# Taking a chunk's sums out of PSUM at the fifth multiplication of the next chunk

## The chip, the cores and the metric

The kernel runs on one core of a Trainium2 chip. A core has five engines with a queue each: PE multiplies matrices, DVE (VectorE) and ACT (ScalarE) work on elements, POOL (GpSimd) here mostly issues gathers, and SP (SyncE) issues transfers. An engine works through its own queue in the order in which the program was written. The metric is the device time in microseconds (us); lower is better.

## The reference

The reference is one layer of a graph network on 6250 nodes with 256 features and 200,000 edges, followed by a mixture of experts and two normalizations. Cut to what matters:

```
h    = x * rsqrt(max(deg_out, 1))                       # every node's row, scaled
m    = segment_sum(h[src], dst) * rsqrt(max(deg_in, 1)) # sum over the edges into each node
x1   = m @ W_gc + b_gc + x @ W_res + b_res
core = top-2 mixture of 64 experts (256 -> 512 -> 256, gelu) of x1
y    = batch-normalized (x1 + core)
out  = layer-normalized (x + y)
```

The edges come sorted by `dst`, and small destinations have many more edges than large ones. The change sits in the `segment_sum`.

## The kernel before, in words

The program first counts degrees, then multiplies `x` by both weights, and keeps the scaled product in SBUF as `hrow`: 50 tiles (`NT`) of 125 nodes, with a value's rounded half in the first 256 columns and the rest in the second 256. Then comes the stage that the change is in, here called the sweep. It sums `hrow` over the edges, in two ways that are written into one another.

**Dense chunks.** The first 1101 groups of 128 edges (`GD`) are split into 30 chunks (`ND`). A chunk covers a window of 128 destination nodes. For a chunk the kernel makes a table of how often each source node occurs for each destination of the window, as follows. DVE makes one-hot tiles from the edge lists, for eight groups at a time: `lo` (L637), `lo` times `worth` with a third part (L642, L643), and `hotk` (L650); all but the `worth` product show as L248, the helper that compares. They are made while the eight groups before are being counted, at the second, fourth and sixth of those (`making`, L652). PE counts a group with one small multiplication `pc<-hotk,lo` (L671), ACT puts a bank of counts into `words` (L655, a "put"), DVE adds the one column that may already hold a count (L706, an "add", written two puts later), and ACT unpacks `words` into `counts` in six pieces (L661, a "cast", of 1024 or 1152 columns). Then PE multiplies `counts` with `hrow`, 50 multiplications of 128 x 512 into one PSUM bank (L715). While chunk c is multiplied, chunk c+1 is counted. The 50 multiplications are the clock of the written order: t goes from 0 to 49 in each chunk, and everything else is placed by t. The six casts for chunk c+1 stand at t = 41, 43, 46 and 48 of chunk c and at t = 1 and t = 4 of chunk c+1 (L879).

**The two banks.** `banks` holds two PSUM banks (`sm`, L597), and chunk c multiplies into bank c % 2. When a chunk's 50 multiplications are done, its sums are taken out into `resd`: ACT scales the second 256 columns into `resd` (L728), DVE scales the first 256 and adds the two (L729), and SP writes `resd` to `z_dram` (L591, in `sums_done`). The bank that is not being multiplied into also serves two small jobs of the same chunk: at t = 20 turned rows of finished nodes go into it (L773) at t = 32 their logits (L782; both earlier and twice in the last two chunks), and at t = 30 a row of totals (L724), which ACT writes into the last two columns of a new `resd` (L725). The totals come from `row_raw`, which SP loads at t = 1 (L718) and DVE turns at t = 24 (L720).

**Gathered chunks.** The other 462 groups of edges are done by fetching 128 rows of `h_dram` each (POOL, L574, a ring of eight buffers), a one-hot tile from DVE (L909) and two multiplications (L579, L580) into a third bank, which ACT copies to `resg` (L932) and SP writes out. They are spread evenly over the written order.

**Finished nodes.** Every chunk also reads back two tiles of nodes whose sums are complete: SP loads `z` and `xr` after t = 20 (L172), DVE makes `x` from them in the next chunk from t = 10 on (L755, L759, L760, L763), PE turns them at t = 20 (L773).

All of the sweep is written by hand under a manual schedule: nothing reorders an engine's instructions. After the sweep come the routing, the 64 experts and the two normalizations, which the change does not touch.

Of the kernel before, what the change touches and what calls it, by code (L numbers as in the profile page):

```python
# [16 lines left out]
AF = mybir.ActivationFunctionType  # L17
ALU = mybir.AluOpType
# [10 lines left out]
NT = N // TP  # L29
D = 256  # L30
# [102 lines left out]
ND = len(DENSE)  # L133
# [21 lines left out]
def gnn_moe_kernel(ctx, tc, x_in, src, dst, bases, nexts, firsts, parts, lasts, runs, W_gc, b_gc, W_res, b_res, Wg, bg, w1, b1, w2, b2,  # L155
                   gamma, beta, out):
    nc = tc.nc
    V, S, G, T = nc.vector, nc.scalar, nc.gpsimd, nc.tensor
# [62 lines left out]
    with tc.tile_pool(name="edges", bufs=1) as ep, ExitStack() as later:  # L221
# [9 lines left out]
        okc = ep.tile([128, ND], F32, name="okc")  # L231
# [29 lines left out]
        with tc.tile_pool(name="late", bufs=1) as lp, tc.tile_pool(name="both", bufs=2) as bp, \  # L261
# [65 lines left out]
            for k, values in enumerate((LOW, HIGH)):  # L327
                c = 0
# [225 lines left out]
        with tc.tile_pool(name="xs", bufs=1) as xs, tc.tile_pool(name="hotg", bufs=2) as hg, \  # L554
# [32 lines left out]
            def sums_done(res, c):  # L587

                row = nc.values_load(base_i[0:1, c:c + 1], engines=(SP_E,), min_val=0, max_val=N,
                                     skip_runtime_bounds_check_because="at most N")  # L590
                nc.sync.dma_start(out=z_dram[ds(row, WIN), :], in_=res)  # L591

            ends_met = {}
            live = {"carry": []}


            banks = [ps_s.tile([128, 512], F32, name=f"sm{i}") for i in range(2)]  # L597
# [114 lines left out]
            def multiply(c, t):  # L712

                sm, ok = banks[c % 2], okc[:, c:c + 1]
                T.matmul(sm, counts[:, t, :], hrow[:, t, :], start=(t == 0), stop=(t == NT - 1))  # L715
                if t == 1:
                    for b in range(3):
                        nc.sync.dma_start(out=row_raw[b * NU:(b + 1) * NU, :], in_=words[c % 2][TP + b:TP + b + 1, :, :])  # L718
                if t == 24:
                    V.tensor_scalar(row_sums, row_raw, -WORD, None, op0=ALU.add)  # L720
                if t == 30:
                    live["resd"] = rsp.tile([WIN, D + 2], F32, name="resd")
                    by = banks[(c + 1) % 2][:, 2 * D - 2:]
                    T.matmul(by, row_sums, two, start=True, stop=True)  # L724
                    S.activation(live["resd"][:, D:], by, AF.Copy, scale=ok)  # L725
                if t == NT - 1:
                    res = live["resd"]
                    S.activation(res[:, :D], sm[:, D:], AF.Copy, scale=ok)  # L728
                    V.scalar_tensor_tensor(res[:, :D], sm[:, :D], ok, res[:, :D], op0=ALU.mult, op1=ALU.add)  # L729
                    ends_met["dense"] = res  # L730
                    if c < ND - 1:
                        sums_done(res, c)

            def last_rows():

# [111 lines left out]
            def dense():  # L847
# [27 lines left out]
                for c in range(ND):  # L875
                    for t in range(NT):
                        for us, g in todo.get(NT * c + t, []):
                            yield us, lambda g=g: count(g)
                        for at, p in ((41, 0), (43, 1), (46, 2), (48, 3), (51, 4), (54, 5)):  # L879
                            d = c + 1 if at < NT else c  # L880
                            if t == at % NT and 0 < d < ND:
                                yield 0.0, lambda d=d, p=p: apart(d, cuts[p], cuts[p + 1])
                        if c == 0 and t % 2 == 0 and made_of < NT:
                            yield 1.0, lambda t=made_of: halves(t)
                            made_of += 2
                            if made_of > NT:
                                yield 0.0, lambda: first_rows()
                        if c == 0 and t == 45:
                            yield 0.0, lambda: left_edges()
                        yield 0.22, lambda c=c, t=t: multiply(c, t)  # L890
                        if 10 <= t < 46:
                            yield 0.04, lambda c=c, t=t: x_step(c, t)
# [70 lines left out]
            with tc.For_i(0, n_groups, 1) as gi:  # L963
# [6 lines left out]
                                op1=ALU.mult)  # L970
# [3 lines left out]
                                       op0=ALU.mult, op1=ALU.add)  # L974
# [22 lines left out]
                with tc.For_i(0, n_win, 1):  # L997
# [9 lines left out]
                    res = rsp.tile([WIN, D + 2], F32, name="res_e", tag="resg")  # L1007
# [82 lines left out]
    with tc.tile_pool(name="xw", bufs=1) as xw, tc.tile_pool(name="xl", bufs=3) as xl, \  # L1090
# [42 lines left out]
        with tc.manual_schedule():  # L1133
# [11 lines left out]
            for t0, z in sums.items():  # L1145
# [7 lines left out]
                for t in range(t0, t0 + n):  # L1153
                    V.scalar_tensor_tensor(x[:, t, :], z[:, t - t0, :D], s_in[:, t - t0:t - t0 + 1], x[:, t, :],
                                           op0=ALU.mult, op1=ALU.add)
# [75 lines left out]
    with tc.tile_pool(name="ps_r", bufs=1, space=PSUM) as ps_r, tc.manual_schedule(engines={PE_E}):  # L1231
# [45 lines left out]
        while n > 2:  # L1277
# [6 lines left out]
                               op1=ALU.mult, accum_out=slots_of)  # L1284
# [285 lines left out]
    with tc.tile_pool(name="fin", bufs=1) as fp, tc.tile_pool(name="gat", bufs=7) as gp, \  # L1570
# [10 lines left out]
        for t0 in range(0, NT, 2):  # L1581
            yr = gp.tile([TP, 2, 2, D], F32, name="yr")
            node_dma(nc.sync, True, yr.rearrange("p t j d -> p t (j d)"), node_rows(y_rows, t0, 2))
            for t in range(t0, t0 + 2):
                for j in range(2):
                    V.scalar_tensor_tensor(x[:, t, :], yr[:, t - t0, j, :], gates[:, j, t:t + 1], x[:, t, :],  # L1586
                                           op0=ALU.mult, op1=ALU.add)
# [23 lines left out]
        scale = fp.tile([TP, D], F32, name="scale")  # L1611
# [121 lines left out]
```

## Time and profile before

| what | us |
|---|---|
| three runs | 1549.29, 1552.34, 1556.32 |
| their median | 1552.34 |
| the profiled execution | 1550.04 |
| span of its instructions | 1548.3 |
| the sweep's 30 chunks, first multiplication to last | about 203 to 912 of the span |

The profiled execution lies 2.3 us below the median, and 1.7 us of it lie outside the span. A row of the timeline gives the start, the duration, the engine, the line, what is written from what, the number of instructions merged into the row, and in brackets how long the engine stood idle before and what ended that. A row of the waits gives who waited for whom, the sum in us, the number of times and the longest. The views that the prediction rests on are shown there.

### The profile page before, as it was taken

Reading aid. Unit: us, or ns where it says so; the run is one execution under the profiler, and the core shown is the slowest. Engines: PE = TensorE matmul, PEld = TensorE weight load, DVE = VectorE, ACT = ScalarE, POOL = GpSimd, SP = SyncE. Lnnn points to the kernel's source line nnn. Section 1 sums busy time; section 2 is a strip of 40 time slices with the busy share of each in tenths; the row PEclk is TensorE's granted clock in tenths of the full one; section 3 lists DMA queues with packets and bytes.
Section 4 is the critical chain, followed back from the end, with each engine's and each line's share of the span. In section 5 each row is a group of like instructions: output and inputs, shape, how many; then the busy total and the mean of one; then the engine's idle time right before and its main releaser. Section 6 shows DMA issues by size and latency. Waiting matters only on the chain. (4 is left out here: it accounts for less than half of the span.)

```text
span 1548.3 us, 27873 instructions
## 1 busy us (share of the span) xinstructions
PE 1370.5 (89%) x8598; PEld 1024.6 (66%) x8598; DVE 978.0 (63%) x2430; ACT 637.9 (41%) x1531; POOL 813.8 (53%) x878
## 2 busy tenths in 40 slices
PE   4999648888899999999999866599999999997995
PEld 2555325556677777777777644588788887886652
DVE  8999878877777877666666538632233223222887
ACT  2343353344465455555555431422222233332247
POOL 5100005777777777777777720256566676663000
PEclk8999858999999999999999975799999999999997
DMA  6789776777878888878787829378789798785934
GB/s 169 225 261 282 223 234 203 198 213 208 233 224 234 231 239 235 231 220 235 229 238 230 242 77 204 92 224 288 213 254 308 229 304 262 247 269 166 236 81 146
DMA packets 215784, 341.92 MB, mean 221 GB/s; under 512 B 23741, under 2 KB 149303, under 8 KB 215627
## 3 DMA queue, kind: packets, MB, share of 16 engines
q1 hardware_dynamic: 159351, 180.34, 40.0%
q0 software_dynamic: 49376, 152.63, 33.8%
q10 hardware_dynamic: 6900, 7.08, 1.6%
q8 instruction: 71, 1.16, 0.3%
q14 instruction: 86, 0.70, 0.2%
HBM read 258.97 MB, written 73.81 MB: 215 GB/s over the span
## 5 line engine op out<-in xcount | busy, mean ns | idle before, releaser
L574 POOL DMA_INDIRECT r<-h_dram,srcg x462 | 503.4, 1090 | 207.2 <-issue 64.3
L715 PE MATMUL sm<-hrow,counts 125*128 125x512 f32 x1500 | 509.1, 430 | 3.4 <-ACT counts L661 3.4
L715 PEld LDWEIGHTS sm<-hrow,counts 125*128 125x128 f32 x1500 | 256.3, 195 | 29.7 <-issue 9.1
L655 ACT ACTIVATE words<-pc 128x136 f32 (+15 forms) x436 | 139.8, 321 | 290.9 <-PE pc L671 275.3
L1433 ACT ACTIVATE hT<-ph,b1c 128x128 f32<-128x128 f32 (+3 forms) x256 | 108.3, 423 | 296.8 <-PE ph L1431 274.5
L671 PE MATMUL pc<-hotk,lo 128*128 128x136 bf16 (+10 forms) x1101 | 183.3, 252 | 48.2 <-DVE hotk L248 42.3
L1431 PE MATMUL ph<-xgT,w1s 128*128 128x128 f32 (+8 forms) x1024 | 207.0, 348 | 0.8 <-DVE xgT L1416 0.8
L1468 PE MATMUL py<-w2s,hT 128*128 128x256 f32 (+1 forms) x800 | 191.9, 383 | 0.0
L661 ACT CAST counts<-words 125x1152 fp32r<-125x1152 uint8 (+1 forms) x180 | 190.7, 1084 | 1.1 <-DVE words L706 1.1
L1431 PEld LDWEIGHTS ph<-xgT,w1s 128*128 128x128 f32 x1024 | 170.9, 192 | 28.8 <-issue 8.6
L1392 POOL DMA_INDIRECT y_dram<-ys,dest x124 | 120.3, 970 | 116.8 <-DVE ys L1446 59.3
L1392 POOL DMA_INDIRECT xg<-x_dram,ids x124 | 121.4, 979 | 102.3 <-DVE ids L1348 64.8
L671 PEld LDWEIGHTS <-lo 128*128 128x128 bf16 x1101 | 74.2, 103 | 133.1 <-issue 90.8
L579 PE MATMUL pg<-r,hot 128*128 128x258 f32 x462 | 146.0, 316 | 18.1 <-DMA r<-h_dram,srcg 17.0
L1468 PEld LDWEIGHTS py<-w2s,hT 128*128 128x128 f32 (+1 forms) x800 | 144.2, 188 | 20.2 <-issue 0.3
L1446 DVE TENSOR_TENSOR ys<-py,b2s 128x256 f32<-128x256 f32 (+3 forms) x124 | 52.4, 423 | 164.6 <-PE py L1468 138.9
L580 PE MATMUL pg<-r,hot 128*128 128x256 f32 x462 | 130.3, 282 | 0.0
L1416 DVE COPY xgT<-pte 128x256 f32<-128x256 f32 (+8 forms) x64 | 38.5, 601 | 135.9 <-PE pte L1414 135.9
L248 DVE TENSOR_TENSOR hotk<-key,iota 128x1088 bf16<-128x1088 bf16 (+10 forms) x138 | 118.9, 862 | 2.6 <-issue 2.6
L579 PEld LDWEIGHTS pg<-r,hot 128*128 128x128 f32 x462 | 88.4, 191 | 41.1 <-DMA r<-h_dram,srcg 28.6
L248 DVE TENSOR_TENSOR lo<-lo_b,iota 128x1000 bf16<-128x1000 bf16 x138 | 93.3, 676 | 28.1 <-PE pc L671 25.8
L428 PE MATMUL pr<-wcat,fT 128*125 128x512 f32 x200 | 102.5, 637 | 3.5 <-DMA wcat<-in_L_gnn_W_res_dram 2.7
(337 smaller groups left out, 1859.5 us busy)
## 6 DMA issues: line engine op xcount, KB each, us to landing
w1s<-in_L_gnn_w_dram SPq DMA_DIRECT2D x64, 512.0 KB
w2s<-in_L_gnn_w_dram SPq DMA_DIRECT2D x64, 512.0 KB
y_dram<-zeros SPq DMA_DIRECT2D x48, 256.0 KB
yr<-y_dram SPq DMA_DIRECT2D x25, 448.0 KB
b2s<-in_L_gnn_b_dram SPq DMA_DIRECT2D x64, 128.0 KB
r<-h_dram,srcg POOLq DMA_INDIRECT x462
h_dram<-hrow SPq DMA_DIRECT2D x5, 1344.0 KB
z_dram<-zeros ACTq DMA_DIRECT2D x7, 903.0 KB
```

The costliest lines, as they stand in the source:

```text
L248: V.tensor_tensor(o, pairs(t, c0, n, m), iota_2[:, None, :m, :].to_broadcast([128, n // 2, m, 2]), ALU.is_equal)
L574: G.indirect_dma_start(out=f32(r[:, :2 * D]), out_offset=None, in_=h_dram[:, :], in_offset=bass.IndirectOffsetOnAxis(ap=idx, axis=0))
L579: T.matmul(pg, hot, r[:, D:], start=first, stop=False)
L580: T.matmul(pg[:, :D], hot, r[:, :D], start=False, stop=last)
L655: return S.activation(to, pc, AF.Copy, bias=WORD)
L661: S.copy(counts[:, t0:t1, :], each[:TP, u:u + t1 - t0, :, b])
L671: T.matmul(pc, los[g // PAIRS][:, r // 2, :, r % 2], hots[g // PAIRS][:, r // 2, :NU * w, r % 2], start=(i == 0), stop=(i == k - 1))
L715: T.matmul(sm, counts[:, t, :], hrow[:, t, :], start=(t == 0), stop=(t == NT - 1))
L1392: w = G.indirect_dma_start(**kw)
L1431: T.matmul(ph[:, :m], w1s[:, kk, c * 128:(c + 1) * 128], xgT[:, kk, :m], start=(kk == 0), stop=(kk == 1))
L1433: S.activation(hT[:, c, :m - apart], ph[:, :m - apart], AF.Gelu, bias=b1_e[:, c:c + 1])
L1468: T.matmul(py[:n], hT[:, c, k * 128:k * 128 + n], w2s[:, c, :], start=(c == 0), stop=(c == 3))
```

## The change

The three steps that take a chunk's sums out (ACT, DVE, SP) become a function `taken`. It is called for chunk c-1 right behind the fifth multiplication (t = 4) of chunk c, and for the last chunk behind its own last multiplication as before. The work itself is the same.

```diff
-                if t == NT - 1:
-                    res = live["resd"]
-                    S.activation(res[:, :D], sm[:, D:], AF.Copy, scale=ok)
-                    V.scalar_tensor_tensor(res[:, :D], sm[:, :D], ok, res[:, :D], op0=ALU.mult, op1=ALU.add)
-                    ends_met["dense"] = res
-                    if c < ND - 1:
-                        sums_done(res, c)
+                if t == 4 and c:
+                    taken(c - 1)
+                if (c, t) == (ND - 1, NT - 1):
+                    taken(c)
+
+            def taken(c):
+                sm, ok, res = banks[c % 2], okc[:, c:c + 1], live["resd"]
+                S.activation(res[:, :D], sm[:, D:], AF.Copy, scale=ok)
+                V.scalar_tensor_tensor(res[:, :D], sm[:, :D], ok, res[:, :D], op0=ALU.mult, op1=ALU.add)
+                ends_met["dense"] = res
+                if c < ND - 1:
+                    sums_done(res, c)
```

In the changed kernel the ACT step is L733 and the DVE step L734; lines behind them are five higher than before. The end of chunk 24 (counting from 0) shows what moves. ACT's queue there before, with casts (L661) and puts (L655) around the step that fills `resd` from the bank `sm`:

```order
L655 ACTIVATE words0_2914<-pc_11102 128x17x14
L661 CAST counts_2916<-words1_2915 125x1152
L661 CAST counts_2916<-words1_2915 125x1024
L728 ACTIVATE resd_11024<-sm0_2944,okc_93 128x256
L655 ISA
L655 ACTIVATE words0_2914<-pc_11124 128x17x14
L661 CAST counts_2916<-words1_2915 125x1024 x2
```

And the same place of ACT's queue now:

```order
L655 ACTIVATE words0_2914<-pc_11102 128x17x14
L661 CAST counts_2916<-words1_2915 125x1152
L661 CAST counts_2916<-words1_2915 125x1024
L655 ISA
L655 ACTIVATE words0_2914<-pc_11118 128x17x14
L661 CAST counts_2916<-words1_2915 125x1024 x2
L733 ACTIVATE resd_11024<-sm0_2944,okc_93 128x256
```

The step has gone behind one put and the last two casts. DVE's queue at the same boundary before, where `lo`, `third` and `hotk` are the one-hot tiles and L706 are the adds:

```order
L706 TENSOR_TENSOR words0_2914<-pc_11038,words1_2915 128x17
L729 SCALAR_TENSOR_TENSOR resd_11024<-sm0_2944,okc_93,resd_11024 128x256
L642 TENSOR_TENSOR lo1_2947<-lo1_2947,worth_90 128x4x250
L248 TENSOR_TENSOR lo1_2947<-third_89,iota_2_73 128x4x6
L706 ISA
L706 TENSOR_TENSOR words0_2914<-pc_11082,words0_2914 128x17
L248 TENSOR_TENSOR hotk_11149<-key_88,iota_2_73 128x2040
```

And now:

```order
L706 TENSOR_TENSOR words0_2914<-pc_11038,words1_2915 128x17
L642 TENSOR_TENSOR lo1_2947<-lo1_2947,worth_90 128x4x250
L248 TENSOR_TENSOR lo1_2947<-third_89,iota_2_73 128x4x6
L706 ISA
L706 TENSOR_TENSOR words0_2914<-pc_11082,words0_2914 128x17
L734 SCALAR_TENSOR_TENSOR resd_11024<-sm0_2944,okc_93,resd_11024 128x256
L248 TENSOR_TENSOR hotk_11149<-key_88,iota_2_73 128x2040
```

Here the step has gone behind two pieces of `lo` and one add, and stands directly ahead of the `hotk` of the next eight groups. On SP the write of `resd` to `z_dram` stood ahead of the load of `row_raw`:

```order
L172 DMA xr2_10964<-r_dram_59 13x2x256
L589 TENSOR_LOAD base_i_95
L591 ISA
L591 DMA z_dram_58<-resd_11024 128x258
L718 DMA row_raw_2948<-words1_2915 17x1x128 x3
```

Now it stands behind it, and the load no longer has a write that waits for DVE in front of it:

```order
L172 DMA xr2_10964<-r_dram_59 13x2x256
L718 DMA row_raw_2948<-words1_2915 17x1x128 x3
L589 TENSOR_LOAD base_i_95
L591 ISA
L591 DMA z_dram_58<-resd_11024 128x258
```

PE's and POOL's queues hold the same instructions in the same order as before.

## The prediction

> **What bounds the kernel now.** I read the page first, then the sweep's stretch alone, then who waits for whom in that stretch, and last the timelines of the three engines at the chunk ends.
>
> ```profile
> span 1548.3 us, 27873 instructions
> PE 1370.5 (89%) x8598; PEld 1024.6 (66%) x8598; DVE 978.0 (63%) x2430; ACT 637.9 (41%) x1531; POOL 813.8 (53%) x878
> 250.00:915.00 665.00, 623.17 (x3693) 473.20 (x3690) 464.28 (x1422) 331.79 (x716) 498.50 (x458) 0.99 0.77 220
> ```
>
> The third line is the stretch in which all chunk ends lie: its length, then busy time of PE, PEld, DVE, ACT and POOL, the granted clock, the DMA share and GB/s. PE is busy for 623 of 665 us, so the sweep is PE's, and what this change can win or lose there is PE's waiting. The waits of that stretch (sum, times, longest):
>
> ```profile
> DVE resd L729 <- ACT resd L728: 91.0, 30, 9.6
> PE pg L579 <- DMA r<-h_dram,srcg: 17.0, 33, 1.7
> DVE row_sums L720 <- DMA row_raw<-words: 15.3, 10, 3.8
> PE pc L671 <- DVE hotk L248: 14.5, 16, 1.7
> PE sm L773 <- DVE xr L763: 5.8, 3, 4.4
> ```
>
> DVE stands still for 91.0 us in front of the step that the change moves, three us at each of 30 chunk ends. PE itself waits 14.5 us for one-hot tiles (`hotk`) that DVE makes, and all but about 1 us of that falls in the six us behind a chunk's end. So the stall on DVE does reach PE, though only a sixth of it. Behind the end of chunk 24, ACT, then DVE, then PE:
>
> ```profile
> 810.26 2.10 ACT L661 CAST counts<-words 125x1152 fp32r<-125x1152 uint8 x2
> 812.25 0.48 ACT L728 ACTIVATE resd<-sm,okc 128x256 f32<-128x256 f32 x1
> 812.62 0.38 ACT L655 ACTIVATE words<-pc 128x238 f32 x1
> 812.86 2.01 ACT L661 CAST counts<-words 125x1024 fp32r<-125x1024 uint8 x2
> 814.75 0.42 ACT L655 ACTIVATE words<-pc 128x238 f32 x1
> ```
>
> ```profile
> 809.02 0.18 DVE L706 TENSOR_TENSOR words<-pc,words 128x17 f32<-128x17 f32 x1
> 812.76 0.48 DVE L729 SCALAR_TENSOR_TENSOR resd<-sm,okc,resd 128x256 f32<-128x256 f32 x1 [3.56 <-ACT resd L728]
> 813.16 0.67 DVE L642 TENSOR_TENSOR lo<-lo,worth 128x1000 bf16<-128x1000 bf16 x1
> 813.75 0.16 DVE L248 TENSOR_TENSOR lo<-third,iota 128x24 bf16<-128x24 bf16 x1
> 813.83 0.18 DVE L706 TENSOR_TENSOR words<-pc,words 128x17 f32 x1
> 813.92 1.22 DVE L248 TENSOR_TENSOR hotk<-key,iota 128x2040 bf16<-128x2040 bf16 x1
> ```
>
> ```profile
> 809.61 1.08 PE L715 MATMUL sm<-hrow,counts 125*128 125x512 f32 x4
> 811.02 1.34 PE L715 MATMUL sm<-hrow,counts 125*128 125x512 f32 x5
> 814.10 0.29 PE L671 MATMUL pc<-hotk,lo 128*128 128x255 bf16 x1
> 815.19 0.27 PE L671 MATMUL pc<-hotk,lo 128*128 128x255 bf16 x1 [0.80 <-DVE hotk L248]
> ```
>
> PE ends the chunk's last multiplication at 809.61 + 1.08 = 810.69 and the fifth of the next chunk at 812.36. ACT comes to L728 only at 812.25, and not because of PE: it has no idle time noted in any of the five rows. It is working off the casts, of which six of about 1 us each stand between t = 41 and t = 4. So what DVE waits for at a chunk end is ACT's backlog of casts, and the sums themselves have long been ready.
>
> **The change part by part.** On ACT the step goes behind one or two puts and the last two casts. At chunk 24 the queue in front of it then ends with the cast pair. That pair ended at 812.86 + 2.01 = 814.87, and ends some 0.37 us earlier (812.62 less 812.25, what L728 took of the queue), at 814.5. The moved step starts there, lasts 0.48, and DVE's half of 0.48 follows: DVE is let go at about 815.45. Before, it had passed that point of its queue at 813.92, when `hotk` began. In between it gains nothing that lasts: freed at 809.2, it does the two `lo` pieces and one add (0.67 + 0.16 + 0.18, overlapped some 0.8 us) and stands again, for more than four us instead of 3.56. So `hotk` is 1.5 us later, ends at 816.65 instead of 815.14, and PE, which came for it at 814.39 (815.19 less 0.80), waits 2.3 instead of 0.8 us. This chunk end costs 1.5 us more.
>
> Not all chunk ends are like that. Chunk 15 is of the other kind:
>
> ```profile
> 630.39 1.06 ACT L661 CAST counts<-words 125x1024 fp32r<-125x1024 uint8 x1
> 629.18 0.48 DVE L729 SCALAR_TENSOR_TENSOR resd<-sm,okc,resd 128x256 f32<-128x256 f32 x1 [3.73 <-ACT resd L728]
> 630.94 1.00 DVE L248 TENSOR_TENSOR hotk<-key,iota 128x1632 bf16<-128x1632 bf16 x1
> 631.99 0.26 PE L671 MATMUL pc<-hotk,lo 128*128 128x204 bf16 x1 [1.55 <-DVE hotk L248]
> ```
>
> Here a `hotk` lies between the old place and the new one. DVE makes it without the 3.73 us of idle time, it is ready before PE asks at 630.44, and the 1.55 us go. The last cast ends at 631.45, so DVE is let go at about 632.0, when it had come to the same point before: nothing is given back. And chunk 19, where PE had no wait at all:
>
> ```profile
> 711.77 2.00 ACT L661 CAST counts<-words 125x1024 fp32r<-125x1024 uint8 x2
> 712.08 0.18 DVE L706 TENSOR_TENSOR words<-pc,words 128x17 f32 x1
> 714.96 1.12 DVE L248 TENSOR_TENSOR hotk<-key,iota 128x1904 bf16<-128x1904 bf16 x1
> 716.56 0.39 PE L671 MATMUL pc<-hotk,lo 128*128 128x238 bf16 x2
> ```
>
> DVE passed the new place at 712.26; now the casts end at 713.77 - 0.37 = 713.4, the two halves of the step take it to 714.35, and DVE is 2.1 us late. Its rows up to `hotk` follow each other without idle time, so `hotk` ends at 718.2 instead of 716.08, and PE, whose second of the two multiplications needs it at 716.7, waits about 1.5 us. Cover that hid the step before (0.6 us between `hotk` and its use) is used up.
>
> I read all 29 chunk ends in that way (the first and the last step are in the row below; the last chunk's own step does not move).
>
> ```profile
> L729 DVE SCALAR_TENSOR_TENSOR resd<-sm,okc,resd x30: 482/484/486, 251.9 to 912.9; 128x256 f32<-128x256 f32 x30
> ```
>
> At eight of them a `hotk` on which PE waits lies between the two places; these waits sum to 10 us (chunk ends 0, 3, 5, 8, 13, 15, 16, 21). At the eight, the next `hotk` is then late by the same reckoning, since PE arrives earlier and DVE about 0.6 us later: about 9 us come back, so the kind as a whole yields 1 us. One end, of chunk 28, has no counting behind it: nothing. At the other 20, DVE is let go 1.3 us later on average (from 0.5 to 2.2), and the next `hotk` had about 0.35 us to spare: 20 x (1.3 - 0.35) = 19 us more of waiting. Sum: 19 - 1 = 18 us. Of that I take off 2 us for chunks 1 to 5, where the 17.0 us of waits for gathered rows mostly lie: there a later PE finds its rows ready. That leaves +16 us.
>
> The other edits. DVE and ACT issue the same instructions with the same durations: nothing. On SP, the three loads of `row_raw` lose the write in front of them and come earlier, so most of the 15.3 us that DVE waits at t = 24 goes; PE's `hotk` waits lie at chunk ends and not there, so I put it at nothing, at most a us of gain. The write of `resd` comes about 2 us later. The reads of `z` that stand behind it are issued after t = 20:
>
> ```profile
> 813.27 0.37 SPq L591 DMA_DIRECT2D z_dram<-resd  x1
> 822.05 0.81 SPq L172 DMA_DIRECT2D z<-z_dram  x2
> ```
>
> With 8.8 us between them, and 2 of these gone, the cover holds; nothing. The bank that is emptied later is next written at t = 20 (L773), which is held by the `xr` rows already (5.8 us in 3 times, above), and by t = 20 the step is five us past: nothing. But `xr` itself is made by the late DVE, so L773 may wait; between 0 and 5 us, the size of that wait now, and I take 0, because PE is late by about as much.
>
> [...]
>
> **Bounds.** The least: DVE's lateness is caught up everywhere but the 10 us at the eight ends go, -10. The most: the lateness reaches PE in full, 20 x 1.3 = 26, nothing is won at the eight ends, and L773 adds 5: +31. I take the working at single ends, +16: 1550.04 + 16 = 1566 for an execution like the profiled one. The median of the runs shown, 1552.34, lies 2.3 us above it, so 1568.
>
> **The rivals.** About 0.5%, or 7.8 us, is what a measurement of this kernel can tell from no change.
>
> *It evens out.* The mechanism: ACT gets through its casts sooner than reckoned, so that DVE is let go only 0.4 us later on average. The eight ends then bring 10 us and give back 4, the other 20 cost 20 x 0.1 or so, as 0.35 us are spare; -4, and with `xr` late +5, so 1548 to 1553. For it: several ends (2, 20, 21) have spare time. Against: casts and puts follow without idle time in the rows above. Chance 0.17. [...]
>
> *Faster.* The wait goes without one that takes its place: DVE finds ACT's half ready at the new place. All 14.5 us of `hotk` waits go: 1538. It decides if ACT's last cast is done before DVE comes by. The casts' rows say that it ends two us after PE's fifth multiplication, when DVE has only about one us of work to do since the old place, so 0.07.
>
> *Much slower.* The adds behind the step hold the five banks of counts, and PE waits for a bank as well. DVE stands for over four us, and the puts above are two us apart (812.62, 814.75), so three of the five banks are held at most; it would be some 0.5 us more at each of 28 ends, and +30: 1582. Chance 0.08.
>
> **How the numbers follow.** The forecast has 0.68, from 1560 to 1578. Slower: 0.68 + 0.08, less what could fall just inside the half per cent, 0.75; no difference 0.18; faster 0.07. The range leaves out the faster case, half of the much slower one and a part of the even one: 1551 to 1582, which holds 0.8 or a little more.
>
> **What would show it.** In the changed profile: ACT's step should follow the last cast without a gap; DVE's wait for it (91.0) should grow to 110 to 125 us, and not shrink; PE's waits for `hotk` in the sweep should go from 14.5 to about 30 us, gone where a `hotk` is made before the step and new where it stands right behind; the waits for `row_raw` should nearly vanish. A DVE wait below 60 us, or `hotk` waits below 15 us, would prove me wrong, and so would a difference outside the sweep.

## The result, and the profile after

The changed kernel takes 1569.38 us (median of five runs, 1565.57 to 1575.77), the kernel before 1552.34 (five runs, 1549.29 to 1560.67): a ratio of 1.0117, with a 95% interval from 1.0087 to 1.0147. Timed a second time, it was 1570.68 against 1552.74, a ratio of 1.0107 (1.0066 to 1.0147). The change makes the kernel 17 to 18 us slower. The prediction was 1568, slower.

The profiled execution of the changed kernel took 1575.77 us, the slowest of its five, and its instructions span 1574.1 us. First the stretch from the first to the last multiplication of the sweep, in before, in after, and in the profile that was taken with the second timing (called after again): length, busy time of PE, PEld, DVE, ACT and POOL, granted clock, DMA share, GB/s.

```profile
202.00:913.00 711.00, 652.75 (x3838) 491.95 (x3838) 499.99 (x1520) 356.01 (x772) 503.37 (x462) 0.97 0.77 220
```

```profile
202.00:939.00 737.00, 658.80 (x3838) 495.64 (x3838) 501.66 (x1521) 355.84 (x772) 505.70 (x462) 0.96 0.75 212
```

```profile
202.00:934.00 732.00, 660.91 (x3838) 497.08 (x3838) 500.26 (x1520) 355.15 (x772) 509.02 (x462) 0.95 0.75 214
```

The windows are drawn around the sweep, which lasts 26 us more in after and 21 us more in after again; the two executions took 25.7 and 19.1 us more than the one of before. So next to nothing was lost or won outside the sweep. The instructions and the busy times of DVE and ACT are the same. PE has two new costs: it stands still for longer (711.00 - 652.75 = 58 us before, 737.00 - 658.80 = 78 us after), and it is busy 6 to 8 us longer with the same 3838 instructions, at a lower granted clock. Who waits for whom from 250 us on, in after:

```profile
DVE resd L734 <- ACT resd L733: 106.3, 30, 12.7
PE pc L671 <- DVE hotk L248: 31.1, 26, 2.8
PE pg L579 <- DMA r<-h_dram,srcg: 17.1, 28, 2.1
PE sm L778 <- DVE xr L768: 7.1, 7, 3.1
PE pc L671 <- DVE words L706: 1.1, 2, 0.9
```

and the same in after again:

```profile
PE pc L671 <- DVE hotk L248: 31.0, 27, 2.8
PE pg L579 <- DMA r<-h_dram,srcg: 14.9, 24, 2.0
```

Read against the same rows of before: DVE's wait for ACT's half of the step grew from 91.0 to 106.3 us, PE's waits for `hotk` from 14.5 to 31.1, and the 15.3 us of waits for `row_raw` have no row any more. The waits for gathered rows and for `xr` hardly moved (17.0 to 17.1 or 14.9, and 5.8 to 7.1). The books of the profiled execution: 16.6 us of `hotk`, 1.3 of `xr`, 1.1 of `words`, which are new, 0.1 of gathered rows and 6.1 of busy time make 25.2 of the 25.7 us.

The end of chunk 24, ACT first, then DVE, then PE:

```profile
827.54 1.99 ACT L661 CAST counts<-words 125x1024 fp32r<-125x1024 uint8 x2
829.43 0.49 ACT L733 ACTIVATE resd<-sm,okc 128x256 f32<-128x256 f32 x1
```

```profile
829.95 0.49 DVE L734 SCALAR_TENSOR_TENSOR resd<-sm,okc,resd 128x256 f32<-128x256 f32 x1 [5.45 <-ACT resd L733]
830.35 1.21 DVE L248 TENSOR_TENSOR hotk<-key,iota 128x2040 bf16<-128x2040 bf16 x1
```

```profile
824.64 1.08 PE L715 MATMUL sm<-hrow,counts 125*128 125x512 f32 x4
831.61 0.27 PE L671 MATMUL pc<-hotk,lo 128*128 128x255 bf16 x1 [2.19 <-DVE hotk L248]
831.64 1.03 PE L715 MATMUL sm<-hrow,counts 125*128 125x512 f32 x2
```

ACT comes to L733 right behind its last cast, without idle time. DVE, which has done the `lo` pieces and an add ahead of it, stands for 5.45 us. `hotk` begins 830.35 - 825.72 = 4.63 us behind the chunk's last multiplication, where it was 813.92 - 810.69 = 3.23 before, and PE waits 2.19 us in place of 0.80. The last row is a surprise: two multiplications take 1.03 us, where they took 0.71 in before:

```profile
815.22 0.71 PE L715 MATMUL sm<-hrow,counts 125*128 125x512 f32 x2
```

The granted clock (the third number from the end) behind three chunk ends in after, 24 to 26:

```profile
831.60:835.50 3.90, 3.89 (x14) 2.86 (x14) 3.86 (x13) 0.60 (x2) 2.03 (x3) 0.56 0.72 186
859.00:863.00 4.00, 4.00 (x17) 3.24 (x16) 2.30 (x8) 1.10 (x3) 2.84 (x3) 0.57 0.81 240
879.00:883.00 4.00, 4.00 (x15) 3.00 (x14) 3.16 (x9) 0.55 (x2) 1.90 (x2) 0.58 0.68 191
```

PE came out of a wait of 1.85 to 2.19 us and ran for some 4 us at a mean clock of little more than half. An estimate from these rows is 3.9 x 0.44 + 4.0 x 0.43 + 4.0 x 0.42 = 5.1 us; by it, each of these three waits cost almost twice its length. That is of the size of the 6.1 us of busy time, but no full account of them: in after the clock is also 0.50 from 446.1 to 453.0 us, where a wait for gathered rows of 2.15 us ends at 446.70, and before has falls of its own, which the last section shows.

### The profile page after: what moved, and what is told of

The parts are those of the page before. It is cut to its first block, busy times and chain, and to the rows that moved or that the text cites. A ratio compares the mean times of both kernels' runs of the same rounds, so it can differ in the third digit from the quotient of the medians.

```text
span 1574.1 us, 27910 instructions
## 1 busy us (share of the span) xinstructions
PE 1375.0 (87%) x8598; PEld 1028.9 (65%) x8598; DVE 977.9 (62%) x2430; ACT 638.0 (41%) x1531; POOL 817.3 (52%) x878
## 5 line engine op out<-in xcount | busy, mean ns | idle before, releaser
L715 PEld LDWEIGHTS sm<-hrow,counts 125*128 125x128 f32 x1500 | 257.8, 196 | 37.8 <-issue 16.6
L655 ACT ACTIVATE words<-pc 128x136 f32 (+15 forms) x436 | 139.7, 321 | 289.5 <-PE pc L671 272.5
L661 ACT CAST counts<-words 125x1152 fp32r<-125x1152 uint8 (+1 forms) x180 | 189.9, 1082 | 2.6 <-PE sm L715 1.5
L579 PE MATMUL pg<-r,hot 128*128 128x258 f32 x462 | 147.0, 318 | 18.8 <-DMA r<-h_dram,srcg 17.1
L706 DVE TENSOR_TENSOR words<-pc,words 128x17 f32 (+1 forms) x435 | 78.9, 181 | 45.8 <-ACT words L655 37.3
```

The costliest lines, as they stand in the source:

```text
L579: T.matmul(pg, hot, r[:, D:], start=first, stop=False)
L655: return S.activation(to, pc, AF.Copy, bias=WORD)
L661: S.copy(counts[:, t0:t1, :], each[:TP, u:u + t1 - t0, :, b])
```

## The experiments

In the expectations, theory A is the prediction's: ACT reaches its half of the step only behind its casts, DVE stands in its queue behind that, and the next `hotk` and PE with it are late. A rival, B, is the other thing that the change moves: SP writes `resd` later and loads `row_raw` ahead of it. Another, C, is that the bank with the sums is held longer, or is read while the other bank is written. A later rival, once A's gains did not come, is that the gathered rows take over as the bound.

Three chips were used, and a kernel is compared only with before on the same chip. On two of them before itself takes 1648.56 and 1631.91 us, and on one 1552.74, close to the 1552.34 of the prediction's runs. Times are medians; a ratio is estimated from all executions and need not be the quotient of two medians.

| kernel | before there | time | ratio (95%) |
|---|---|---|---|
| DVE's half alone later | 1648.56 | 1647.05 | 0.9982 (0.9958 to 1.0007) |
| the whole step at t = 9 | 1648.56 | 1647.29 | 0.9992 (0.9962 to 1.0021) |
| the write alone later | 1648.56 | 1651.09 | 1.0018 (0.9991 to 1.0046) |
| the last two casts behind the step | 1648.56 | 1649.33 | 1.0012 (0.9982 to 1.0043) |
| after, again | 1552.74 | 1570.68 | 1.0107 (1.0066 to 1.0147) |
| DVE's half alone later, again | 1552.74 | 1552.57 | 0.9990 (0.9962 to 1.0018) |
| the whole step at t = 9, again | 1552.74 | 1553.03 | 1.0006 (0.9984 to 1.0029) |
| the last two casts behind the step, again | 1552.74 | 1555.45 | 1.0007 (0.9978 to 1.0035) |
| the whole step at t = 3 | 1631.91 | 1639.99 | 1.0047 (1.0018 to 1.0076) |
| after, with `hotk` made earlier | 1631.91 | 1638.03 | 1.0026 (1.0002 to 1.0050) |

**DVE's half alone later.** ACT's half stays at t = 49, where it was before. DVE's half and the write go to t = 4, as in after. All edits up to the fetches are to after. The three new functions hold the three steps of `taken`, one each; their definitions are left out here.

```diff
                 if t == 4 and c:
-                    taken(c - 1)
-                if (c, t) == (ND - 1, NT - 1):
-                    taken(c)
+                    added_half(c - 1)
+                    written(c - 1)
+                if t == NT - 1:
+                    scaled_half(c)
+                    if c == ND - 1:
+                        added_half(c)
```

> ACT's half of the step stays at the chunk's last multiplication (in front of the last two casts), DVE's half and the write go to t = 4. Theory A (DVE stands behind ACT's casts, and the one-hot tiles behind it come late): DVE is let go no later than before at any chunk end, so the waits of PE for hotk in the sweep fall from 14.5 us of before to 2 to 6 us, and the time to 1541, 1536 to 1548. Rival B (the write of resd and what SP reads behind it come late): as after, 1569. Rival C (the bank is held longer or is read while the other is written): DVE's read of the bank is as late as after, so 1560 to 1569.

**The whole step at t = 9.** Behind the tenth multiplication instead of the fifth.

```diff
-                if t == 4 and c:
+                if t == 9 and c:
```

> The whole step at t = 9 instead of t = 4, so behind the place where ACT has worked off its casts. Theory A: DVE's wait for ACT's half falls from 106 us to under 40, PE's hotk waits in the sweep from 31 to 10 us or less, time 1540 to 1550, below before. Rival B: the write is later still, so 1569 or more. Rival C: the bank is held longer still, 1569 or more.

**The write alone later.** Both halves at t = 49 as before, and only `sums_done` at t = 4.

```diff
                 if t == 4 and c:
-                    taken(c - 1)
-                if (c, t) == (ND - 1, NT - 1):
-                    taken(c)
+                    written(c - 1)
+                if t == NT - 1:
+                    scaled_half(c)
+                    added_half(c)
```

> Both halves stay at the chunk's last multiplication, and only SP's write of resd goes to t = 4, behind the load of row_raw. Theory A: hotk waits 14 to 15 us as before, DVE's wait for row_raw nearly gone, time as before, 1552 within 5. Rival B: 1565 to 1569. Rival C: as before, 1552.

**The last two casts behind the step.** After, with the casts of t = 1 and t = 4 put at t = 8 and t = 12.

```diff
-                        for at, p in ((41, 0), (43, 1), (46, 2), (48, 3), (51, 4), (54, 5)):
+                        for at, p in ((41, 0), (43, 1), (46, 2), (48, 3), (58, 4), (62, 5)):
```

> The step stays at t = 4 as in the changed kernel, but the last two casts go from t = 1 and t = 4 to t = 8 and t = 12, behind it. Theory A: ACT comes to the step about 2 us sooner, DVE's wait for it falls from 106 to 40 to 75 us, hotk waits from 31 to 4 to 12 us, time 1538 to 1552, a little more if the casts now hold up the x rows. Rivals B and C: the write and the emptying of the bank stand where they stood, so 1565 to 1569.

These four ran on the chip where before takes 1648.56 us, and none of them differs from before by more than the measurement tells. After itself was not timed on that chip, so whether it shows the loss at all is not known. In the profile of the first of them:

```profile
DVE words L706 <- issue: 37.0, 36, 4.0
PE pc L671 <- DVE hotk L248: 26.9, 20, 4.2
PE pg L579 <- issue: 14.6, 9, 2.8
```

DVE and PE stand still for up to 4 us at a time with nothing that the profile shows as the reason ("issue"), and waits for `hotk` may come from that too. These waits did not fall as expected: they are 26.9, 36.6 and 27.0 us in the first, second and fourth of these kernels. The write alone later costs nothing that can be measured there (1.0018, 0.9991 to 1.0046); that gives B no support, but on such a chip it is a weak test, and it was not repeated on the other one. The other three were, together with after:

> The changed kernel itself, as a control beside the three below, since the four kernels tried first ran where the kernel before took 1648.56 instead of 1552.34. Theory A (DVE stands behind ACT's casts, and the one-hot tiles behind it come late): 1.009 to 1.015 of before where before takes about 1552; where every engine has waits that the profile does not explain, as there, 1.000 to 1.010, since those waits give DVE time to catch up. Rivals B and C: 1.009 to 1.015 in both.

> ACT's half of the step at the chunk's last multiplication, DVE's half and the write at t = 4, a second time. Theory A: 0.990 to 0.998 of before, PE's hotk waits in the sweep 2 to 6 us. Rival B (late write): as the changed kernel. Rival C (bank held longer): 1.005 or more.

> The whole step at t = 9, a second time. Theory A: DVE's wait for ACT's half under 40 us, hotk waits 10 us or less, 0.992 to 1.000 of before. Rivals B and C: as the changed kernel or slower.

> The step at t = 4 and the last two casts behind it, at t = 8 and t = 12, a second time. Theory A: DVE's wait 40 to 75 us, hotk waits 4 to 12 us, 0.991 to 1.000 of before. Rivals B and C: as the changed kernel.

After is slower there by 1.07%, and each of the three edits takes the whole loss away. The waits of DVE's half alone later:

```profile
DVE resd L739 <- ACT resd L735: 48.5, 21, 13.5
PE pg L579 <- DMA r<-h_dram,srcg: 26.0, 41, 1.8
PE sm L785 <- DVE xr L775: 4.3, 1, 4.3
PE pc L671 <- DVE hotk L248: 3.4, 5, 1.0
```

of the last two casts behind the step:

```profile
PE pg L579 <- DMA r<-h_dram,srcg: 27.9, 41, 2.3
PE sm L778 <- DVE xr L768: 5.8, 2, 5.0
PE pc L671 <- DVE hotk L248: 3.1, 5, 1.0
```

and of the whole step at t = 9:

```profile
PE pg L579 <- DMA r<-h_dram,srcg: 23.1, 37, 1.8
PE pc L671 <- DVE hotk L248: 9.8, 15, 1.4
PE sm L778 <- DVE xr L768: 8.2, 8, 5.2
```

The first two kernels show A: the same DVE step at the same t = 4 costs 17 us or nothing, and what decides is whether casts stand ahead of ACT's half. DVE and PE have the same instructions in the same order in both as in after; only ACT's order and the times differ. The third rules out B and C. In it DVE's half starts 4.5 us behind a chunk's last multiplication on average and the write 5.2 us, in after 3.9 and 4.5; both are later still, and nothing is lost. At the end of chunk 24 `hotk` is made there ahead of the step that waits:

```profile
812.32 1.22 DVE L248 TENSOR_TENSOR hotk<-key,iota 128x2040 bf16<-128x2040 bf16 x1
818.12 0.48 DVE L734 SCALAR_TENSOR_TENSOR resd<-sm,okc,resd 128x256 f32<-128x256 f32 x1 [1.85 <-ACT resd L733]
```

In the first two, with ACT free of the casts, the waits for `hotk` fall to 3.4 and 3.1 us, below the 14.5 of before. What A also expected, a kernel some 11 us faster than before, did not come: 0.9990 and 1.0007. The 11 us are in the rows, though not as a gain. The waits for gathered rows rose from 17.0 to 26.0 and 27.9. Added up, the three waits of PE are 14.5 + 17.0 + 5.8 = 37.3 us before, 33.7, 36.8 and 41.1 in the three kernels, and 55.3 in after. The times go with these sums rather than with the `hotk` waits alone, by which the three would be 5 to 11 us faster than before. The sums set after apart; they do not order the other four, whose times differ by no more than the measurement tells.

Why the rows take over can be read from POOL. Its fetches between 205 and 890 us in before, in after and in DVE's half alone later (number; busy us and mean ns of one; idle us ahead of them and what ended it), and two fetches of the last:

```profile
L574 POOL DMA_INDIRECT r<-h_dram,srcg x461 | 502.4, 1090 | 201.0 <-issue 64.3 <-DMA h_dram<-hrow 57.9 <-PE pc L671 33.7
L574 POOL DMA_INDIRECT r<-h_dram,srcg x445 | 488.9, 1099 | 215.3 <-issue 61.9 <-DMA row_raw<-words 57.3 <-PE pg L580 44.4
L574 POOL DMA_INDIRECT r<-h_dram,srcg x461 | 504.5, 1094 | 197.5 <-issue 60.3 <-DMA row_raw<-words 57.4 <-PE pc L671 34.1
```

```profile
866.21 0.97 POOL L574 DMA_INDIRECT r<-h_dram,srcg  x1 [0.30 <-PE pg L580]
867.48 0.95 POOL L574 DMA_INDIRECT r<-h_dram,srcg  x1 [0.30 <-PE sm L715]
```

POOL issues one fetch behind the other, with 0.30 us between two of them whatever is named behind the arrow. The 57 us in front of a DMA are one wait ahead of the first fetch, which starts at 244 us in all three. Without it, the mean pause is (197.5 - 57.4) / 461 = 0.304 us in DVE's half alone later, 0.310 in before and 0.355 in after. So in DVE's half alone later the 461 fetches stand back to back, 461 x (1.094 + 0.304) = 644 us from 244 to 889, and before was only 461 x 0.006 = 3 us away from that. At each of PE's 41 waits for rows there, the fetch had started 3.6 us or more behind the use that made its buffer free, and 0.30 or 0.31 us behind the fetch ahead of it: what it waited for was POOL's queue. By these rows, no other place of the step can gain much more than the 3 us while POOL has that queue.

**One in six fetches left out.** To see whether the rows are what holds the gain back, both orders were run with a sixth of the fetches left out: the ring's buffer is then multiplied with the rows that it still holds. The sums are then not the reference's, and with such sums the stages behind the sweep take over 10,000 us longer, so only the sweep is read, and the expected times of the whole kernel cannot be held against it. The first kernel is DVE's half alone later with

```diff
-                if n + NR < len(rows):
+                if n + NR < len(rows) and n % 6:
```

> ACT's half at the chunk's last multiplication and DVE's half at t = 4, and one in six of the fetches of gathered rows left out (the multiplications then use the rows that the buffer still holds). Question: where the 11 us of hotk waits went that this order saved without a gain in time. If they went into waits for gathered rows (17 of before, 26 there), these fall below 6 us here, hotk waits stay at 3 to 6 us, and the time is 1526 to 1538, 8 to 12 us below the next kernel. If something else took them, the two kernels take the same time within 3 us.

and the second the kernel before with the same edit.

> The kernel before, with the same one in six of the fetches left out. Waits for gathered rows fall from 17 to below 6 us, hotk waits stay at 14 to 20 us, time 1536 to 1548.

Their whole times are 12263.61 and 12293.55 us. The sweep of the first, and PE's waits in it from 250 us on:

```profile
203.00:890.00 687.00, 639.81 (x3838) 490.86 (x3838) 502.06 (x1519) 353.52 (x772) 434.42 (x386) 0.97 0.71 198
```

```profile
PE pc L671 <- DVE hotk L248: 10.6, 11, 3.8
PE pc L671 <- issue: 6.9, 8, 2.3
```

and of the second:

```profile
203.00:910.00 707.00, 646.53 (x3838) 493.52 (x3838) 499.34 (x1521) 354.93 (x772) 423.13 (x386) 0.97 0.69 193
```

```profile
PE pc L671 <- DVE hotk L248: 22.5, 18, 3.0
PE pc L671 <- issue: 5.0, 9, 1.2
```

With 386 fetches no wait for gathered rows is listed, and the order that gained nothing with all fetches now makes the sweep 707 - 687 = 20 us shorter, with 12 us less of waits for `hotk`. The `hotk` waits are above what was expected (10.6 for 3 to 6, 22.5 for 14 to 20). That fits a gain that the fetches held back, but it does not show it. Neither order was run with all fetches on this chip; on the chip of 1648.56 us, where DVE's half alone later has no listed wait for rows either, that order gained nothing (0.9982). And these are one profile each, from a chip with "issue" waits. So the 20 us are a sign and no measurement, and that the fetches are the bound rests on POOL's queue above.

**The step at t = 3, and `hotk` earlier.** Two more on that chip: after with the step one multiplication earlier, ahead of ACT's last cast,

```diff
-                if t == 4 and c:
+                if t == 3 and c:
```

> The whole step at t = 3 instead of t = 4, so in front of the last cast and behind the fifth. Theory A (DVE stands behind ACT's casts): one cast of 1.0 us less stands in front, so DVE is let go about 1 us earlier at each end; PE's hotk waits in the sweep fall from 31 to 12 to 20 us and the time to 1553 to 1562. Rivals B and C: one multiplication earlier changes nothing, 1567 to 1571.

and after with the one-hot tiles made at the second, third and fourth of eight groups in place of the second, fourth and sixth.

```diff
-            making = {1: lo_of, 3: worth_of, 5: hot_of}
+            making = {1: lo_of, 2: worth_of, 3: hot_of}
```

> The changed kernel, with the one-hot tiles of the next eight groups made one and two counts earlier (worth at the third, hotk at the fourth of the eight instead of the fourth and the sixth). Theory A: DVE waits for ACT as long as in the changed kernel, 95 to 110 us, but the tile has 1.5 to 3 us more to spare, so PE's hotk waits fall from 31 to 3 to 12 us and the time to 1550 to 1558. Rivals B and C (late write, bank held): nothing of theirs moves, 1567 to 1571.

Step at t = 3:

```profile
PE pc L671 <- DVE hotk L248: 44.9, 29, 4.7
```

`hotk` earlier:

```profile
PE pc L671 <- DVE hotk L248: 17.6, 15, 3.8
```

The expectations were in times of the chip of 1552.74 us, and after was not timed on this one, so both are inconclusive as to after. Both are a little slower than before (1.0047 and 1.0026). The waits for `hotk` are above what A expected in both, 44.9 us for 12 to 20 and 17.6 for 3 to 12; the first does not support A, and that `hotk` made earlier has far fewer of them fits A, and no more than that.

## Why the prediction was right

**ACT reaches the step behind its casts: shown.** The timeline has L733 behind the last cast without idle time, and taking the casts away from ahead of it (by leaving ACT's half at t = 49, or by putting two casts behind it) undid the loss.

**DVE is let go later: right in place, a little too high in its sum.** At chunk 24 `hotk` was to be 1.5 us later; it is 4.63 - 3.23 = 1.40. The wait was to grow to 110 to 125 us and is 106. In chunk 24 it grew from 3.56 to 5.45.

**The single ends.** Chunk 24: 2.3 us of waiting forecast, 2.19 measured. Chunk 15, where the wait was to go with nothing given back:

```profile
638.63 1.00 DVE L248 TENSOR_TENSOR hotk<-key,iota 128x1632 bf16<-128x1632 bf16 x1
642.57 0.48 DVE L734 SCALAR_TENSOR_TENSOR resd<-sm,okc,resd 128x256 f32<-128x256 f32 x1 [2.85 <-ACT resd L733]
641.24 0.36 PE L671 MATMUL pc<-hotk,lo 128*128 128x204 bf16 x2
```

`hotk` is made ahead of the step and ready at 639.63; PE's row, the pair whose second stood for 1.55 us, has no idle time. Chunk 19, which was to wait 1.5 us where it had not waited:

```profile
727.14 0.36 PE L579 MATMUL pg<-r,hot 128*128 128x258 f32 x1 [0.37 <-issue]
729.65 0.27 PE L671 MATMUL pc<-hotk,lo 128*128 128x238 bf16 x1 [0.73 <-DVE hotk L248]
```

It waits 0.73, and 0.37 us of idle time ahead of that, which is named "issue", has used up some of the rest.

**The sum of the `hotk` waits: right.** Of the forecast +18 us, +16.6 are measured (14.5 to 31.1). By kind, adding up the waits in each chunk (those too short for the listing included, 0.3 us before): the 20 costly ends went from 3.8 to 23.2 us, +19.4 where +19 was forecast. The eight ends with a `hotk` in between went from 11.0 to 7.9, -3 where -1 was forecast (one of the eight, 5, had no wait in before). The end of chunk 28 has none in either.

**Gathered rows, -2:** 17.0 to 17.1 in one profile, to 14.9 in the other; too small to tell. **`xr`, 0 of at most 5:** +1.3 and +0.2. **`row_raw`:** the waits are gone and bought nothing, as forecast. **Nothing outside the sweep:** right.

**What the sum left out** is the clock. It priced a wait of PE at its own length; the waits of about 2 us at chunks 24 to 26 cost another 1.7 us each, by the estimate above. With 6.1 us of busy time, the 2 us at the gathered rows that were not won, 2.4 of `xr` and `words`, and 1.4 less of `hotk`, the +16 become the 25.2 us of the books. The median came out at 1569.38, 1.4 us from the forecast, and that it is so close is in part luck: it is so because the execution that was profiled is 6.4 us above its median and that of before 2.3 below its own: 25.7 - 6.4 - 2.3 = 17.0. The four other executions of after were granted a clock of 0.943 to 0.947, the profiled one 0.941. The profile of after again, 1.5 us below its median, lies 19.1 us above that of before.

**The rivals.** "It evens out" needed the 20 costly ends to cost some 2 us in all, and they cost 19.4. "Much slower" needed waits of PE for a bank of counts at 28 ends. The 1.1 us that PE waits for `words` are of that kind, since that add frees a bank of counts, but they are 2 waits. "Faster", with all `hotk` waits gone, was priced at 1538; its mechanism did not happen in after. In the kernel with DVE's half alone later it nearly did (3.4 us left) and the time was 1552.57, so its price was wrong as well: it left out that POOL's queue of fetches is the next bound, 3 us away.

After has no row in which PE waits for a bank of sums to be emptied, and is 17 us slower all the same: PE waits behind DVE's queue, 31.1 us for `hotk` where it was 14.5.

## What to carry to other kernels

For an evacuation that two engines share, look at what the first of them has queued, and not only at when the bank is needed: the second stands in its own queue for all that lies ahead of the first. Here DVE stood for 106.3 us in after and 91.0 in before, and for 48.5 with ACT's half ahead of the last casts and its own half later. Before pricing the end of a wait at its full length, look for the next bound and how far it is: here 11 us of saved waits came back as 9 to 11 us of waits for rows, because the fetches stand back to back on their own queue from 244 to 889 us. And a new wait of PE can cost more than its length: here the waits of 1.85 to 2.19 us behind chunks 24 to 26 were followed by some 4 us at a mean granted clock of 0.56 to 0.58.

## What the hardware showed that was not expected

The granted clock fell behind waits of 1.85 to 2.19 us, though not each time: in after it stayed at 1.00 behind one of 2.16 us that ended at 289.96. The 0.56 to 0.58 above are means: cut finer, the clock in after is 0.50 from 831.85 to 835.26 us, for 3.41 us, and 1.00 on both sides. Before has such falls too, one of them behind waits for gathered rows of 1.03 and 0.65 us:

```profile
333.77:337.19 3.42, 3.42 (x16) 2.22 (x14) 0.25 (x2) 0.55 (x2) 2.51 (x4) 0.50 0.92 290
```

Between 250 and 905 us the clock falls to 0.50 twice in before and five times in after. Five of the seven falls last 3.41 or 3.42 us, the other two 6.83.

In after, the wait of 2.85 us behind chunk 11 was followed by a full clock; in after again the same wait, of 2.8 us, by half. The clock around the two waits, in after and in after again, in stretches as long as the fall:

```profile
551.97:555.38 3.41, 2.27 (x15) 1.86 (x14) 1.27 (x5) 2.65 (x5) 2.50 (x4) 1.00 0.81 201
555.38:558.79 3.41, 1.70 (x10) 1.48 (x11) 3.33 (x10) 0.55 (x2) 0.84 (x1) 1.00 0.84 266
558.79:562.21 3.42, 3.42 (x23) 3.00 (x22) 3.42 (x10) 1.42 (x4) 2.79 (x3) 1.00 0.39 85
```

```profile
552.51:555.92 3.41, 0.95 (x5) 0.91 (x6) 3.36 (x10) 0.29 (x3) 1.28 (x2) 1.00 0.87 273
555.92:559.33 3.41, 3.41 (x14) 2.81 (x13) 3.38 (x11) 0.71 (x3) 1.27 (x2) 0.50 0.31 68
```

In after the wait is spread over two of these stretches, in which PE is busy for 2.27 and 1.70 us. In after again nearly all of it lies in one, with 0.95 us busy, and the next one runs at half the clock. What decides whether a wait is followed by a fall is not shown: no run was made to test it.

On the same kernel, two of the three chips take 5 and 6% longer than the third (1631.91 and 1648.56 against 1552.74 us). These two show idle time on DVE and PE that ends with nothing recorded, up to 4.0 and 2.8 us in the rows above. Why is open.
